# Causal maxima of four heads in four 32-row groups, three PSUM bank pairs, and the order of the steps as tables

## The chip, the core and the metric

The kernel runs on one core of a Trainium2 chip. The time is the device time of one execution in microseconds, the median of three runs. One execution was recorded by the hardware profiler; all rows below are from it. In its rows PE is TensorE's matmuls and PEld its weight loads, DVE is VectorE, ACT ScalarE, POOL GpSimd, and SP the queue that issues the DMAs.

## What is computed

Two transformer layers work on a tensor of 8 batches, 512 tokens and 128 channels. Every part normalises its input per token and adds its output to the residual.

1. A linear attention with 16 heads of 64 channels (`K` and `Q` are `elu + 1`, their sums over the tokens, a reciprocal, an output projection, a gelu).
2. A feed-forward part with three weights of 352 x 128, whose inputs and weights are quantised to FP4 in blocks of 16 and put back.
3. A causal softmax attention with 16 heads of 8 channels:

```python
a = jnp.einsum('bqhd,bkhd->bhqk', q, k) / Dh ** 0.5
a = jnp.where(jnp.tril(jnp.ones((1, 1, Lq, Lq), bool)), a, NEG_INF)
a = jax.nn.softmax(a, axis=-1)
o = jnp.einsum('bhqk,bkhd->bqhd', a, v)
```

4. A mixture of eight experts of low rank, of which two are chosen for each token.

The change is in part 3, and in how the instructions of all parts are ordered.

## The kernel before

**A plan.** The functions of `block_kernel` don't issue instructions. Through `nc` (an `Nc` over a `Plan`, lines 135 to 408) every call becomes a step with its engine, or `either`, which may be VectorE or GpSimd. `Plan.ordered` (line 249) then runs the steps in a model with a cost for each (`cost`, line 613), a rank for each stage (`TURNS`, line 706) and a pool of slots for each kind of tile. It picks for each engine the ready step of lowest rank, and so sets the order on every queue, the slot of every tile and the engine of every `either` step. `one_go` makes several calls one step, `together` lets a run of matmuls wait for all that they need. `kept_warm` (line 365) puts matmuls with zeros (`plan.warmer`, line 907) into gaps of TensorE that the model has. `Plan.issue` (line 397) emits the result. All of these instructions have line 407 in the profile, so the rows are told apart by tile.

**Stages.** For each batch: `normed_T`, `linear_attention` with `linear_out`, `fp4_feed_forward`, `causal_attention`, `routed`, `experts` (loop at line 1496). Stages of different batches are mixed. The elementwise products of `products` (`r`, `qf`), `quantised` (`qa`, `xf`, `hq`), `linear_out` (`y`) and `experts` (`act`, `um`) are `either` steps, 392 in all.

**PSUM.** Eight banks: two pairs (`pair`, 2 x 512 floats), one bank `mid` for the product with the values, three banks `ahead` for all else. `ahead` may also borrow halves of a pair.

**The causal attention.** Heads go in groups of four, 32 groups in all (`NG` = 4 a batch). A group's queries and keys lie in two tiles `qkT`, called `duo(n, i)` for `i` = 0, 1, in each of which head `h` = 0, 1 stands at partitions 64`h` to 64`h` + 31 (`stack`, line 1191). The 32 rows are high and low parts of 8 channels. `spread` (line 1195) loads them from HBM, where `projected` put them.

`group(n)` (line 1286) has two parts mixed in one loop over four blocks `t` of 128 tokens. For the next group, `largest` (line 1210) computes the maximum over the keys for each query: matmuls of 32 rows over the first 128(`t` + 1) keys, a matmul that adds the mask `mask_q` (a 128 x 128 bfloat16 tile of 0 and -1e30, multiplied by an identity) to the block on the diagonal, and a reduction on VectorE straight from PSUM. For t = 0 and 1 all four heads fit in one pair; for t = 2 and 3 two tiles take a pair each, one after the other (`shared`, line 1206). `to_queries` (line 1236) turns the maxima, in two parts, into two rows that are stored by DMA under the queries at partitions 64`h` + 32 and 33, so that the scores come out of the matmul with the maximum subtracted. For its own group, `scores` (line 1255) has matmuls over these 34 rows, an exponential on ScalarE (`pr`), and a select on GpSimd that clears what lies above the diagonal; then four matmuls with the values go side by side into four column groups of `mid`.

```python
for at, i in enumerate(some):
    for h in range(2):
        nc.tensor.matmul(heads[:, h, at, :], duo(n, i)[stack(h), 0, ts(t, P)],
                         duo(n, i)[stack(h), 1, 0:w], start=(at == 0), stop=False, ...)
for h in range(2):
    nc.tensor.matmul(heads[:, h, :, ts(t, P)], ident16,
                     mask_q.unsqueeze(1).to_broadcast([P, k, P]), start=False, stop=True, ...)
```

`first_maxima` (line 1342) fills the `qkT` tiles' key halves with ones and makes the maxima of group 0.

Of the kernel before, what the change touches and what calls it, by code (L numbers as in the profile page):

```python
# [9 lines left out]
F32 = mybir.dt.float32  # L10
F32R = mybir.dt.float32r
BF16 = mybir.dt.bfloat16
U32 = mybir.dt.uint32
AF = mybir.ActivationFunctionType
# [97 lines left out]
class Buf:  # L112


    def __init__(self, tag=None, place=None):
        self.tag, self.place = tag, place
        self.writer, self.readers = None, []
        self.first, self.users = None, {}


class Step:


    def __init__(self, number, engine, lane):
        self.number, self.engine, self.rank, self.lane = number, engine, 0.0, lane
        self.calls, self.needs, self.takes, self.uses = [], {}, [], {}
        self.cost, self.slow, self.port, self.size = 0.0, 0.0, False, 0
        self.work = 0.0
        self.start = self.end = None


TWO_PORTS = ("tensor_tensor", "scalar_tensor_tensor", "tensor_scalar", "tensor_copy")


class Plan:
# [3 lines left out]
    HOP = {"tensor": 0.1, "gpsimd": 0.1, "vector": 0.1, "scalar": 0.1, "sync": 0.2}  # L139

    def __init__(self, nc):
        self.nc, self.steps, self.open = nc, [], None
        self.lane, self.tags, self.psum, self.warmer = None, {}, (), None
        self.parts = {}
        self.engines = {n: Engine(self, n) for n in (*self.HOP, "either")}


    def tag(self, name, places, parts=None):

        self.tags[name] = list(places)  # L150
        self.parts[name] = parts or [((name, i),) for i in range(len(places))]
# [24 lines left out]

    def fixed(self, place):
        return View(Buf(place=place), place.shape)

# [4 lines left out]
    def together(self):  # L184
        return Together(self)

    def span(self, lane, low, high):
        return Span(self, lane, low, high)

    def add(self, engine, method, a, k):  # L190
        step = self.open
        if step is None:
            step = Step(len(self.steps), engine, self.lane)
            self.steps.append(step)
        elif step.engine is None:
            step.engine = engine
        assert step.engine == engine
        out = [k["out"]] if "out" in k else [a[0]]
        ins = [x for x in (*a[0 if "out" in k else 1 :], *k.values()) if isinstance(x, View)]
        if k.get("accum_out") is not None:  # L200
            out.append(k["accum_out"])
        step.calls.append((method, a, k))
        fast = "vector" if engine == "either" else engine
        if method is not None:
            step.cost += cost(fast, method, out[0], ins, a, k)
        if engine == "tensor" and method is not None:
            step.work += work(method, ins, a, k)
        if engine == "sync":
            step.size += 4 * out[0].shape[0] * _free(out[0])
        if engine == "either":  # L210
            step.slow += cost("gpsimd", method, out[0], ins, a, k)

        if engine == "gpsimd" and method != "memset":
            step.port = True
        elif engine in ("vector", "either") and method in TWO_PORTS:
            two = sum(v.shape[-1:] != (1,) or len(v.shape) > 2 for v in ins) > 1
            step.port |= (two or _free(out[0]) > 16) and not any(
                v.buf.tag in self.psum for v in (*ins, out[0]) if isinstance(v, View)
            )
        for v in ins:  # L220
            if all(v is not o for o in out) and isinstance(v, View):
                self.reads(step, v.buf)
        for v in out:
            if isinstance(v, View):
                self.writes(step, v.buf)

    def reads(self, step, buf):
        assert buf.writer is not None or buf.tag is None
        if buf.writer is not None and buf.writer is not step:
            step.needs[buf.writer] = True  # L230
        buf.readers.append(step)
        self.used(step, buf)

    def writes(self, step, buf):
        for s in (buf.writer, *buf.readers):
            if s is not None and s is not step:
                step.needs[s] = True
        buf.writer, buf.readers = step, []
        if buf.first is None and buf.tag is not None:
            buf.first = step  # L240
            step.takes.append(buf)
        self.used(step, buf)

    def used(self, step, buf):
        buf.users[step] = True
        step.uses[buf] = True


    def ordered(self):

        free = Free(self.parts)
        slots = {}
        left = {s: len(s.needs) for s in self.steps}
        then = {s: [] for s in self.steps}
        for s in self.steps:
            for n in s.needs:
                then[n].append(s)
        users = {}  # L260
        for s in self.steps:
            for b in s.uses:
                users[b] = len(b.users)
        ready_at = {s: 0.0 for s in self.steps}
        empties = set()
        for s in self.steps:
            for b in s.uses:
                if b.tag in self.psum and s.engine != "tensor" and (False or max(b.users, key=lambda u: u.number) is s):
                    empties.add(s)
        waiting = {e: [] for e in self.engines}  # L270
        for s in self.steps:
            if not left[s]:
                waiting[s.engine].append(s)
        turns = {}
        for s in sorted(self.steps, key=lambda s: (s.rank, s.number), reverse=True):
            for b in s.takes:
                turns.setdefault((s.lane, b.tag), []).append(b)
        busy = dict.fromkeys(self.engines, 0.0)
        port = 0.0
        moved = 0.0  # L280
        ends = []
        now, done, order, stuck = 0.0, 0, [], False
        clock = Clock()
        while done < len(self.steps):
            for e in self.HOP:
                while busy[e] <= now:
                    best, kept = None, set()
                    shared = waiting["either"] if e in ("vector", "gpsimd") else []
                    ready = [s for s in (*waiting[e], *shared) if ready_at[s] <= now]
                    ahead = HURRY if e == "tensor" and clock.idle(now) else 0.0  # L290
                    for s in sorted(
                        ready,
                        key=lambda s: (s.rank - (ahead if s.work > 0.6 * s.cost else 0.0) - (EMPTY if s in empties else 0.0), s.number),
                    ):
                        if s.port and port > now:
                            continue
                        asked = {}
                        for b in s.takes:
                            asked.setdefault(b.tag, []).append(b)
                        if not all(  # L300
                            all(b in turns[s.lane, t][-len(bs) :] for b in bs)
                            for t, bs in asked.items()
                        ):
                            continue
                        if all(
                            (t not in kept or stuck) and free.has(t, len(bs)) for t, bs in asked.items()
                        ):
                            best = s
                            break

                        kept.update(asked)
                    if best is None:
                        break
                    if any(
                        now < ready_at[s] <= now + PATIENCE and s.rank < min(best.rank - MARGIN, LIMIT)
                        for s in (*waiting[e], *shared)
                    ):
                        break
                    s, stuck = best, False
                    waiting[s.engine].remove(s)  # L320
                    if s.engine == "either":
                        s.engine = e
                        s.cost = s.slow if e == "gpsimd" else s.cost
                    for b in s.takes:
                        slots[b] = free.take(b.tag)
                        turns[s.lane, b.tag].remove(b)
# [1255 lines left out]
```

## Time and profile before

| | |
|---|---|
| time, median of 3 runs | 1126.88 us (1125.94 to 1127.14) |
| span of the profiled execution, first to last instruction | 1130.1 us, 3.2 us above the median |
| maxima: matmuls 32 rows | 512 instructions |
| maxima: mask matmuls | 384 instructions, 61.6 us busy |
| maxima: reductions `mx<-pair` on VectorE | 192, 198.5 us busy |
| fills with zeros | 88 instructions (44 fills), 40.4 us busy |
| `qf<-qf,r` and `qf<-qf,z`, 128x512, on GpSimd | 128, mean 1.27 us |
| `act<-act,tw`, 128x512, on GpSimd | 64, mean 1.27 us |
| `y<-y,y`, 128x512, on VectorE | 8, mean 0.73 us |
| `sc<-h`, reduction of 128x704, on VectorE | 14, mean 0.88 us |

How to read it: the page gives each engine's busy time, the chain of waits that ended last, and groups of instructions by tile, as `out<-in`. `x4` is a count. An fp32 matmul of 128 rows is two instructions. Matmuls overlap their neighbours, so a matmul's own duration is longer than the distance to the next one's start. The timeline merges like instructions that follow one another into one line with a count. A stretch's granted clock is the share of TensorE's full clock.

### The profile page before, as it was taken

How to read it: one execution, taken by the hardware profiler on the slowest of the kernel's cores; microseconds unless marked ns; L12 is line 12 of the kernel's file. 1: busy time of each engine (PE TensorE's matmuls, PEld its weight loads, DVE VectorE, ACT ScalarE, POOL GpSimd, SP SyncE). 2: the span in 40 equal slices, each digit the busy share in tenths (PEclk: the TensorE clock that was granted, in tenths of full speed). 3: DMA queues.
4: the chain of work that ended last, by engine and by line, in shares of the span. 5: the costliest groups of instructions: out<-in, count | busy, mean ns of one | idle time of the engine just before them, and what ended most of it. 6: DMA issues, size and time to landing. Idle time of an engine off the chain costs nothing.

```text
span 1130.1 us, 15043 instructions
## 1 busy us (share of the span) xinstructions
PE 1040.2 (92%) x5025; PEld 488.0 (43%) x5025; DVE 830.3 (73%) x1868; ACT 630.8 (56%) x1084; POOL 624.3 (55%) x669
## 2 busy tenths in 40 slices
PE   6667788998899999999998999999999999999998
PEld 2223333344344444444543444454454445445454
DVE  6868879897888967758788968788667765556543
ACT  5756787678786644644578555764443443344311
POOL 6647846676676466237635755467644533441534
PEclk9879989999999999999999999999999999999999
DMA  8000030001101020111012000210002102001000
GB/s 235 1 1 0 1 111 1 21 20 56 39 20 30 10 94 20 58 72 35 26 39 94 19 21 20 95 30 19 20 7 98 39 20 104 21 20 30 1 10 9
DMA packets 30572, 44.31 MB, mean 39 GB/s; under 512 B 4192, under 2 KB 18464, under 8 KB 30496
## 3 DMA queue, kind: packets, MB, share of 16 engines
q1 hardware_dynamic: 30496, 43.37, 11.9%
q8 instruction: 39, 0.64, 0.2%
q14 instruction: 37, 0.30, 0.1%
HBM read 23.95 MB, written 18.87 MB: 38 GB/s over the span
## 4 chain that ended last, share of the span: by engine, by line
PE 57%; DVE 15%; ACT 6%; issue 2%; POOL 1%; DMA 0%; POOLq 0%; DVEq 0%; ACTq 0%
PE ahead L407 31%; PE pair L407 19%; PE mid L407 7%; ACT pr L407 2%; DVE r L407 2%; DVE mx L407 2%; DVE h L407 1%; DVE sc L407 1%; ACT qf L407 1%; DVE s4 routing L407 1%; DVE qf L407 1%; DVE act L407 1%; ACT z L407 1%; DVE kf L407 1%; DVE oh L407 1%
## 5 line engine op out<-in xcount | busy, mean ns | idle before, releaser
L407 ACT ACTIVATE pr<-pair 128x1024 f32<-128x1024 f32 (+1 forms) x192 | 166.7, 879 | 149.2 <-PE pair L407 129.1
L407 DVE TENSOR_REDUCE mx<-pair 128x4 f32<-128x512 f32 (+2 forms) x192 | 198.5, 1041 | 68.4 <-PE pair L407 57.7
L407 POOL TENSOR_SCALAR_AFFINE_SELECT pr<-pr 128x256 f32<-128x256 f32 (+1 forms) x192 | 92.8, 485 | 176.4 <-ACT pr L407 175.6
L407 PE MATMUL pair<-qkT 32*128 32x128 f32 (+7 forms) x1024 | 172.3, 387 | 9.4 <-ACT pr L407 2.7
L407 PEld LDWEIGHTS pair<-qkT 32*128 32x128 f32 (+1 forms) x1024 | 84.4, 183 | 181.8 <-ACT pr L407 52.0
L407 POOL TENSOR_TENSOR act<-act,tw 128x512 f32<-128x512 f32 x64 | 81.3, 1272 | 88.8 <-DVE act L407 80.6
L407 PE MATMUL ahead<-um,b_sb 128*128 128x512 f32 x240 | 122.2, 607 | 0.0
L407 DVE RECIPROCAL r<-r 128x256 f32<-128x256 f32 x64 | 110.3, 1736 | 14.9 <-POOL r L407 14.8
L407 DVE SCALAR_TENSOR_TENSOR act<-act,ahead 128x512 f32<-128x512 f32 x120 | 81.9, 684 | 51.4 <-ACT act L407 38.0
L407 POOL TENSOR_TENSOR qa<-qa,qa 128x704 f32<-128x704 f32 (+4 forms) x60 | 81.2, 1354 | 35.1 <-DVE qa L407 26.2
L407 POOL TENSOR_TENSOR qf<-qf,r 128x512 f32<-128x512 f32 x64 | 80.5, 1278 | 34.5 <-DVE r L407 27.8
L407 PE MATMUL mid<-pr,va 128*10 128x512 f32 (+3 forms) x1024 | 93.3, 435 | 0.0
L407 POOL TENSOR_TENSOR qf<-qf,z 128x512 f32<-128x512 f32 x64 | 80.3, 1270 | 0.0
L407 ACT ACTIVATE act<-ahead 128x512 f32<-128x512 f32 x60 | 35.8, 597 | 72.0 <-PE ahead L407 71.9
L407 PE MATMUL ahead<-act,a_sb 128*128 128x512 f32 x128 | 65.2, 619 | 0.0
L407 POOL TENSOR_TENSOR r<-z,z 128x512 f32<-128x512 f32 x32 | 40.9, 1278 | 41.6 <-ACT z L407 39.3
L407 PE MATMUL ahead<-tT,w_sb 128*128 128x512 f32 x120 | 63.3, 609 | 0.0
L407 ACT ACTIVATE ahead<-ahead,bqkv_sb 128x512 f32<-128x512 f32 x96 | 63.0, 656 | 0.0
L407 PE MATMUL pair<-mask_q,ident 128*128 128x128 bf16 (+1 forms) x384 | 61.6, 242 | 0.0
L407 PE MATMUL ahead<-xnT,wk 128*128 128x512 f32 x100 | 56.7, 650 | 4.8 <-DVE kf L407 2.1
L407 PEld LDWEIGHTS ahead<-um,b_sb 128*128 128x128 f32 x240 | 40.7, 190 | 36.1 <-issue 29.6
L407 ACT ACTIVATE z<-qf,eps_sb,s 128x512 f32<-128x512 f32 x64 | 51.9, 811 | 6.8 <-DVE s L407 5.1
(227 smaller groups left out, 1986.4 us busy)
## 6 DMA issues: line engine op xcount, KB each, us to landing
stacks<-qk SPq DMA_DIRECT2D x32, 512.0 KB
qkT<-stacks SPq DMA_DIRECT2D x128, 128.0 KB
x<-in SPq DMA_DIRECT2D x8, 256.0 KB
qkT<-mr SPq DMA_DIRECT2D x128, 4.0 KB
out<-x SPq DMA_DIRECT2D x8, 256.0 KB
w_sb<-in SPq DMA_DIRECT2D x3, 256.0 KB
wq<-in SPq DMA_DIRECT2D x4, 128.0 KB
wk<-in SPq DMA_DIRECT2D x4, 128.0 KB
```

The costliest lines, as they stand in the source:

```text
L407: getattr(e, method)(*a, **k)
```

## The change

**Four row groups.** Head (`i`, `h`) now stands at partitions 64`h` + 32`i` of tile `duo(n, i)`, so the four heads of a group lie in four 32-row groups. `largest` takes two pairs at once, and each head has a bank of its own. It is called for t = 1, 2, 3; the call for t = 1 does t = 0 too, with 384 columns a head, of which the middle 128 are t = 0. The maxima of t = 1 come out in two parts, and `to_queries` joins them with a minimum (the maxima are negated).

```diff
-    def stack(h):
-        return slice(64 * h, 64 * h + 32)
+    def stack(i, h):
+        return slice(64 * h + 32 * i, 64 * h + 32 * i + 32)
...
+        t = max(t, 1)
+        some = (1, 0) if t == 1 else (t,)
+        w = sum((u + 1) * P for u in some)
+        pairs = [new("pair", [P, 2, 512]) for _ in range(2)]
+        four = [(i, h) for h in range(2) for i in range(2)]
+        with one_go():
+            for u in some:
+                for i, h in four:
+                    to, keys = pairs[i][:, h, 0:w], duo(n, i)[stack(i, h), 1, 0 : (u + 1) * P]
...
+                    nc.tensor.matmul(
+                        to, duo(n, i)[stack(i, h), 0, ts(u, P)], keys,
+                        start=(u == t), stop=False, skip_group_check=True,
+                    )
+            k = len(some)
+            for i, h in four:
+                nc.tensor.matmul(
+                    pairs[i][:, h, w - k * P : w].rearrange("p (k c) -> p k c", k=k),
+                    mask_q[stack(i, h)],
+                    mask_k[stack(i, h)].unsqueeze(1).to_broadcast([32, k, P]),
+                    start=False, stop=True, skip_group_check=True,
+                )
+        for i in range(2):
...
+            nc.vector.tensor_reduce(to, heads, AX.X, ALU.max, negate=True)
...
+        nc.vector.tensor_tensor(mx[:, :, 2], mx[:, :, 2], mx[:, :, 0], ALU.min)
```

The rows of the maxima go to the free half of each 64 partitions: 64`h` + 32 for `i` = 0 as before, 64`h` for `i` = 1. There the scores' matmul takes 64 rows, of which 30 hold zeros that `first_maxima` puts there once: the two odd tiles get eight fills in place of two.

```diff
-                        rows = slice(64 * h, 64 * h + 34)
+                        rows = slice(64 * h, 64 * h + (64 if i else 34))
```

**The mask as two factors.** `mask_q` and `mask_k` are bfloat16 tiles of 128 x 128 whose product over 32 rows gives the causal mask; each 32-row group holds the same rows. `causal_factors` makes them at the start, ahead of the other constants, with ten iotas on GpSimd and fifteen steps on VectorE on tiles of at most 150 columns, in one scratch tile (`pr`). It takes the place of a memset and a select on GpSimd.

**PSUM.** Three pairs, one bank `mid`, one bank `ahead`. `ahead` may use the six halves of the pairs.

```diff
-    places("pair", [P, 2, 512], 2, pool=sums)
+    places("pair", [P, 2, 512], 3, pool=sums)
...
-    places("ahead", [P, 512], 3, pool=sums)
+    places("ahead", [P, 512], 1, pool=sums)
```

**Tables.** The model, its costs, ranks and slots are gone. `ORDER` lists the 5108 steps in the order in which they are issued, two signs a step; `ENGINES` names an engine for each of the 392 `either` steps (126 `v`, 266 `g`); `PLACES` gives the slot of each tile; `ZEROS` names 15 fills by their place in the order (36 to 1394) and columns (192 to 512).

```diff
-        plan.issue()
+        plan.issue(ORDER, ENGINES, PLACES, ZEROS)
```

By stage the 126 are: 35 in the linear attention and its gelu, 48 in the FP4 part, 43 in the experts.

## The prediction

> **What bounds the kernel now.** I read the page's busy shares first, then the chain that ended last, then the busy time of each engine in three stretches, then TensorE's timeline inside an attention group.
>
> ```profile
> PE 1040.2 (92%) x5025; PEld 488.0 (43%) x5025; DVE 830.3 (73%) x1868; ACT 630.8 (56%) x1084; POOL 624.3 (55%) x669
> ...
> PE 57%; DVE 15%; ACT 6%; issue 2%; POOL 1%; DMA 0%; POOLq 0%; DVEq 0%; ACTq 0%
> ```
>
> The chain is mostly TensorE, and VectorE comes next. The stretches are cut at the first maxima matmul (172.0 us) and behind the last maxima (1036):
>
> ```profile
> 0.00:172.00 172.00, 126.68 (x313) 54.43 (x313) 129.35 (x348) 117.77 (x210) 106.34 (x130) 0.91 0.19 57
> 172.00:1036.00 864.00, 826.81 (x4385) 391.13 (x4385) 656.79 (x1430) 491.72 (x839) 479.71 (x505) 1.00 0.12 39
> 1036.00:1130.10 94.10, 86.76 (x331) 42.42 (x330) 44.18 (x92) 21.28 (x37) 38.21 (x35) 0.98 0.02 6
> ```
>
> The columns are stretch, length, then busy time of PE, PEld, DVE, ACT, POOL, then the granted clock. Ahead of the attention no engine is full (PE 127, DVE 129 of 172). In the middle TensorE is busy 827 of 864 us: 37 us are left, and another 18.3 us of its busy time are the fills with zeros. All maxima lie in this stretch, so this is where the change has to be priced. VectorE is busy 657 of 864 there (76%).
>
> **Maxima on TensorE.** One group of heads in TensorE's timeline, columns start and duration:
>
> ```profile
> 650.69 0.44 PE L407 MATMUL pair<-qkT 32*128 32x128 f32 x4
> 651.06 0.39 PE L407 MATMUL pair<-mask_q,ident 128*128 128x256 bf16 x2
> 651.29 1.08 PE L407 MATMUL ahead<-aout_sb,oT 128*128 128x128 f32 x8
> ...
> 654.46 0.50 PE L407 MATMUL pair<-qkT 32*128 32x256 f32 x4
> 654.90 0.39 PE L407 MATMUL pair<-mask_q,ident 128*128 128x256 bf16 x2
> ...
> 659.00 0.44 PE L407 MATMUL pair<-qkT 32*128 32x384 f32 x2
> 659.37 0.28 PE L407 MATMUL pair<-mask_q,ident 128*128 128x128 bf16 x2
> 659.49 0.66 PE L407 MATMUL ahead<-wT,hqT 128*128 128x128 f32 x4
> ...
> 662.67 0.50 PE L407 MATMUL pair<-qkT 32*128 32x512 f32 x2
> 663.11 0.28 PE L407 MATMUL pair<-mask_q,ident 128*128 128x128 bf16 x2
> ```
>
> Matmuls are pipelined, so a cost is the distance from one start to the next. Before: t=0 takes 651.06 - 650.69 = 0.37 for scores and 651.29 - 651.06 = 0.23 for the mask, 0.60. t=1 takes 0.44 + 0.23 = 0.67. t=2 takes 0.37 + 0.12 = 0.49, twice, 0.98. t=3 takes 0.44 + 0.12 = 0.56, twice, 1.12. Sum 3.37 us a group, 108 us for 32 groups. Two heads already run beside each other: two matmuls of 512 columns together take the 0.44.
>
> After: the four heads stand in four row groups and four banks. If four run beside each other as two do now, t=3 is 0.44 and t=2 is 0.37; the joined t=1 and t=0 take half of 0.44 and half of 0.37, 0.41. The masks are now four 32-row matmuls of 256, 128 and 128 columns that run together; I give them what two mask matmuls of that width take now, 0.23 + 0.12 + 0.12 = 0.47, though they may take half, 0.23. Sum 0.44 + 0.37 + 0.41 + 0.47 = 1.69 us, a saving of 1.68 x 32 = **54 us**.
>
> Four row groups at once are not in this trace, so both ends: if only two go at a time, scores stay at 0.37 + 0.44 + 0.74 + 0.88 = 2.43, and masks two by two cost 0.47: saving 0.47 x 32 = 15 us. With masks at half, 62 us. A loss on TensorE is excluded by the rows: two row groups do overlap, and no column is added. I take 54, because the nearest rows overlap fully: two row groups here, and four column groups in the product with the values.
>
> The page "TensorE: Matmul & The Clock Gate" of the Trainium skill, "Measured speedup vs the span model", speaks against full overlap: four row tiles at 512 columns gave 3.07 times, not four. By it a four-way step costs 4/3.07 = 1.30 of the trace's overlapped one, an estimate: scores 1.22 become 1.59, and 12 us of the gain are lost.
>
> The scores' matmuls for the odd tile contract 64 rows where they contracted 34; the columns are the same and the row of 34 costs what the row of 32 costs (0.44 at 384 columns): nothing, cover not needed.
>
> **Fills.** Before has 44 (88 instructions, 40.4 us busy, 17.2 / 18.3 / 5.0 in the three stretches); the table has 15, all within the first 1394 of 5108 steps. They stand in gaps, so leaving them out gives nothing by itself and at most 18 in the middle. What they cover is the granted clock (1.00 in the middle); a stretch at 0.86, as at 50 to 100 us, would cost about 14% of itself. TensorE is so full there that I put nothing.
>
> **Elementwise steps.** All 392 steps that may go to either engine run on GpSimd now. The table sends 126 to VectorE: 24 before the first maxima, 91 in the middle, 11 behind. VectorE has no such row with two SBUF tensors but y<-y,y (0.73 us at 512 columns; 0.68 mostly); for 704 columns I take the reduction sc<-h, 0.88. Middle: 71 x 0.73 + 20 x 0.88 = 70 us more on VectorE; GpSimd loses 71 x 1.27 + 20 x 1.5 = 120. The new minimum over two parts is 32 x 0.17 = 5 us (row s4 routing, 128x4); it sits ahead of the maxima's copy and their DMA, a group ahead of use. The number of reductions and their elements per group are equal (5120). So VectorE in the middle goes from 657 to 732. The fullest 50 us that it shows (350 to 400) are 45.85, 92%; at 92% it needs 732 / 0.92 = 796 us. TensorE needs 864 - 54 = 810. TensorE still ends last, by little. Bounds: nothing, if VectorE keeps up, to the second rival's price.
>
> **Start.** The mask's factors are made by 10 iotas and 15 small VectorE steps that alternate through one scratch tile; the old mask took two GpSimd steps. By rows of 0.29 (affine select, 128 columns) and about 0.2 (small VectorE steps), 10 x 0.29 + 15 x 0.2 = 6 us one after another; the six further fills of qkT cost some 2 us (0.36 each for the wide ones). All of it stands ahead of the first statistics at 5.16 on VectorE's queue, and GpSimd's pow is behind the iotas; the weights' loads on SP run meanwhile. Between 0, if it hides behind the first load, and 8; I take 5, as everything waits for the first normalised tile.
>
> **Banks.** The three pairs are a further slot for the maxima and scores; one own bank, and borrowed halves, are left for everything else. Total banks are equal. Now TensorE's loads waited 33.9 us in 52 cases for a reduction and 53.1 us in 91 for an exponential, but TensorE itself stood only 2.0 and 2.7 us for them. Both ends: a quarter of the 55 us of gaps and fills in the middle gained, or the third rival's loss. I take 10 us gained, from the freer pairs and from moved steps that end 0.6 us sooner.
>
> The table's order keeps the stretches' content: the same linear parts of three batches ahead of the first maxima; behind the last maxima all 54 TensorE steps of the last experts and 47 of 54 of the ones before, where the trace now has all of both. So 172 and 94 stay.
>
> **Sum.** 1130.1 - 54 + 5 - 10 = 1071 on the profiled span. That span is 1.003 of the median 1126.9, so 1068.
>
> **Rivals.**
>
> *Better than that.* TensorE gets the 62 us, the start hides, and the gaps and fills of the middle shrink by 30 of 55: 1130 - 62 - 30 = 1038, 1035 on the median's scale. For it: no engine is full in the first 172 us and the steps are freer. Against: VectorE at 657 + 75 = 732 would have to be busy 94% of the 778 us left.
>
> *VectorE becomes the bound.* The copy and subtraction of the maxima show what VectorE suffers beside GpSimd:
>
> ```profile
> L407 DVE CAST m<-mx x32: 174/175/987, 185.6 to 1036.3; 128x16 fp32r<-128x16 f32 x32
> L407 DVE TENSOR_TENSOR m<-mx,m x32: 105/175/1245, 188.2 to 1036.5; 128x16 fp32r<-128x16 f32 x32
> ```
>
> The same 175 ns step takes up to 1.25 us; its mean of 281 ns is 0.11 over the median. GpSimd, with 480 - 120 = 360 us left in some 810, would be busy 44% of the time, and a step that met one of its 1.27 us steps half way waits 0.64: 0.44 x 0.64 = 0.28. At 0.3 us for each of the 91 moved steps VectorE would need (732 + 27) / 0.92 = 825 us: 172 + 5 + 825 + 94 = 1096, 1093. The page "SBUF — State Buffer", "SBUF: two separate sides", says that a VectorE step with two SBUF inputs and a GpSimd step exclude each other for a whole instruction; by it each such wait may last GpSimd's 1.27 us, which fits the maximum of 1.25. If two row groups at a time is all there is, the answer is 1130 - 15 + 5 = 1120, 1117.
>
> *Slower.* Each of the 96 maxima blocks takes two pairs, four of the seven shared banks, and frees the second only when two reductions (0.95 to 1.22 us each) are through. If TensorE then waits for one reduction a block, that is 96 x 1.04 = 100 us: 1130 - 54 + 5 + 100 = 1181, 1178. It decides from a wait of 0.5 us a block on. Against it: the 2.0 us of such waits now, with two pairs only. That the fixed order itself stands badly to the chip would look the same, as waits of TensorE.
>
> **Chances.** Forecast 0.45, better 0.22, VectorE 0.18, two at a time 0.05, slower 0.08, no change 0.02. A measurement of this kernel can tell about 0.2%. Faster 0.90, same 0.02, slower 0.08. The range that leaves out no more than two in ten goes from the better case to beyond the VectorE case: 1031 to 1101.
>
> **What would show it.** Right: the four 32-row matmuls start within some 20 ns, a t=3 block costs 0.5 to 0.6 us in place of 1.12, TensorE's busy time falls to about 955, VectorE's rises to about 925, and GpSimd's falls to about 465. Wrong: four heads that start two by two; TensorE waiting for mx; VectorE above 93% in the middle with TensorE idle behind it; a clock below 0.97 behind 300 us, where no fills are left; a first statistics step after 15 us.

## The result, and the profile after

The changed kernel takes 1267.39 us (median of four runs, 1263.94 to 1273.39) where the one before took 1127.01 beside it: ratio 1.123, 95 % interval 1.118 to 1.127. It is 12 % slower; the forecast was 1068. The profiled execution took 1267.84 us, with a span of 1266.1.

The page of the changed kernel: busy shares, the granted clock in 40 slices, and the chain that ended last.

```profile
PE 1029.0 (81%) x4967; PEld 482.4 (38%) x4967; DVE 913.6 (72%) x2047; ACT 636.3 (50%) x1084; POOL 485.8 (38%) x551
...
PEclk9898979989989999889979998999998889996999
...
PE 20%; DVE 10%; ACT 4%; issue 1%; POOL 1%; DVEq 0%; ACTq 0%; POOLq 0%
```

VectorE (913.6; "about 925") and GpSimd (485.8; "about 465") came out close to the forecast. TensorE did not: 1029.0 us busy in place of 955, at a granted clock that stands below 0.9 in 13 of the 40 slices (3 before), and only 81 % of the span. No engine is full. The chain's known shares add up to 36 %; before, to 81 %.

The three stretches of the changed kernel, cut at its first maxima matmul (194.60) and behind its last maxima (1169); columns as in the prediction.

```profile
0.00:194.60 194.60, 128.99 (x305) 55.82 (x305) 148.39 (x402) 119.28 (x214) 92.04 (x116) 0.89 0.16 49
194.60:1169.00 974.40, 817.31 (x4338) 386.33 (x4341) 717.25 (x1547) 495.85 (x836) 368.26 (x412) 0.92 0.11 35
1169.00:1266.10 97.10, 82.65 (x329) 40.28 (x321) 47.99 (x101) 21.17 (x36) 25.48 (x24) 0.96 0.02 6
```

The loss is in the first two stretches: 194.6 us for 172.0, and 974 for 864. In the middle TensorE stands 157 us (it stood 37), and the clock is 0.92 where it was 1.00. The idle time of TensorE in the waits of the changed kernel (us in total, times, longest):

```profile
PE pair L214 <- DVE act L214: 32.7, 31, 3.2
PE pair L214 <- DVE qf L214: 22.4, 14, 3.5
PE pair L214 <- DVE pair L214: 18.0, 10, 4.4
PE pair L214 <- ACT pr L214: 15.0, 33, 3.1
PE pair L214 <- ACT pair L214: 15.0, 8, 4.1
PE pair L214 <- DVE mx L214: 12.7, 26, 2.2
```

The largest are not the maxima (`mx`, 12.7 us). They are matmuls into a `pair` that wait for a VectorE step that has just *read* a `pair`: the experts' product into `act`, the linear attention's sum into `qf`.

TensorE's time from one start to the next, summed by kind over the records, with its idle time apart (us; "one tile" is the experiment that decided the case, below):

| | before | after | after, one tile |
|---|---|---|---|
| maxima, masks | 77.1, 39.0 | 35.7, 24.2 | 35.3, 23.7 |
| fills | 37.8 | 16.6 | 15.7 |
| all other matmuls | 886 | 951 | 886 |
| idle | 82.3 | 227.7 | 100.3 |
| of it, waits for a reader of the pair's other half | 7 | 121 | 2 |
| busy at half clock, by the clock's records | 33 | 176 | 64 |

So maxima and masks gave up 56 us, as forecast (54). Idle time took 145, and the other matmuls grew by 65, which fits the clock: 176 us of TensorE's busy time ran at half clock (33 before), and (176 - 33) / 2 = 72 us. The row of the other half is worked out as follows: each instruction of the trace was matched with its call in the order table, so that for each matmul it is known when its operands were written, when its own half was last read, and when the other half was. What is counted is time in which TensorE was free, operands and own half were ready, and the start came only when a reader of the *other half* had ended. By the same count such time went from 26 to 60 us on ScalarE and from 22 to 54 on VectorE: readers wait for the other half's writer as well.

One of these, TensorE in the changed kernel:

```profile
835.11 0.59 PE L214 MATMUL pair<-tT,w_sb 128*128 128x512 f32 x1
835.54 1.02 PE L214 MATMUL pair<-um,b_sb 128*128 128x512 f32 x2
839.73 1.39 PE L214 MATMUL pair<-xnT,wv 128*128 128x512 f32 x2 [3.17 <-DVE qf L214]
```

and VectorE at that time:

```profile
835.71 3.35 DVE L214 RECIPROCAL r<-r 128x256 f32<-128x256 f32 x2
838.98 0.10 DVE L214 SCALAR_TENSOR_TENSOR s4 attention<-mv attention,s4 attention 128x4 f32<-128x4 f32 x1
839.00 0.68 DVE L214 SCALAR_TENSOR_TENSOR qf<-pair,qf 128x512 f32<-128x512 f32 x1
```

The projection of the values needs `xnT` and `wv`, ready long since. It goes to half 0 of pair 0, which nobody uses. Half 1 of the same pair waits for VectorE, which is in two reciprocals. TensorE is free from 836.56; the matmul starts at 839.73, 50 ns after `qf` has been read out of half 1. The reading is that the program orders a write to a tile behind the readers of that tile, and that a pair is one tile; "One tile for all of PSUM", below, tests it. The case costs 3.17 us on TensorE, and behind it, from 840.46 on, the clock's records show half clock for 3.4 us.

### The profile page after: what moved, and what is told of

It reads as the page before. It is cut to its first block, busy times and chain, and to the rows that moved or that the text cites. A ratio compares the mean times of both kernels' runs of the same rounds, so it can differ in the third digit from the quotient of the medians.

```text
span 1266.1 us, 14915 instructions
## 1 busy us (share of the span) xinstructions
PE 1029.0 (81%) x4967; PEld 482.4 (38%) x4967; DVE 913.6 (72%) x2047; ACT 636.3 (50%) x1084; POOL 485.8 (38%) x551
## 5 line engine op out<-in xcount | busy, mean ns | idle before, releaser
L214 DVE TENSOR_REDUCE mx<-pair 128x6 f32<-128x768 f32 (+2 forms) x192 | 193.1, 1037 | 44.7 <-PE pair L214 43.1
L214 PE MATMUL pair<-qkT 32*128 32x128 f32 (+11 forms) x1024 | 143.7, 410 | 34.7 <-ACT pr L214 12.9
L214 PEld LDWEIGHTS pair<-qkT 32*128 32x128 f32 (+2 forms) x1024 | 72.2, 197 | 179.7 <-ACT pr L214 56.8
L214 PE MATMUL pair<-um,b_sb 128*128 128x512 f32 x192 | 102.2, 630 | 22.0 <-DVE act L214 15.4
L214 DVE SCALAR_TENSOR_TENSOR act<-act,pair 128x512 f32<-128x512 f32 x96 | 65.0, 683 | 71.5 <-ACT act L214 39.1
L214 PE MATMUL pair<-xnT,wv 128*128 128x512 f32 x106 | 59.8, 650 | 22.5 <-DVE qf L214 11.0
L214 PE MATMUL pair<-xnT,wk 128*128 128x512 f32 x100 | 61.4, 707 | 18.4 <-ACT pair L214 6.3
L214 PE MATMUL pair<-xnT,wq 128*128 128x512 f32 x100 | 57.7, 662 | 16.6 <-DVE pair L214 4.4
L214 PE MATMUL pair<-qf,wk_o 128*128 128x512 f32 x96 | 55.7, 699 | 17.4 <-ACT pair L214 5.5
L214 ACT ACTIVATE pair<-pair,bqkv_sb 128x512 f32<-128x512 f32 x100 | 65.6, 658 | 6.6 <-PE pair L214 5.8
```

The costliest lines, as they stand in the source:

```text
L214: getattr(e, method)(*a, **k)
```

## The experiments

First theories: **tables** (the fixed order stands badly to the chip), **banks** (fewer own banks, blocks that take two pairs), **engines** (the moved elementwise steps) and **clock** (the missing fills). The theory that won, **shared tile**, came out of the first four runs and the trace.

### The change without its tables

The changed maxima, mask factors and banks in the kernel before, whose own planner makes the order and chooses the fills (its costs of the 32-row matmuls are adjusted); all `either` steps run on GpSimd. Then the same with the banks of before.

```diff
-    places("pair", [P, 2, 512], 2, pool=sums)
-    places("ahead", [P, 512], 3, pool=sums)
+    places("pair", [P, 2, 512], 3, pool=sums)
+    places("ahead", [P, 512], 1, pool=sums)
```

> The changed maxima, mask factors and three bank pairs, but ordered by the model of the kernel before (which also picks fills, slots and engines) in place of the tables. Theory 'tables' (the fixed order doesn't fit the chip, so TensorE waits and its clock falls): TensorE waits below 120 us, clock above 0.97, time 1070 to 1110. Theory 'banks' (two pairs at a time and one own bank make TensorE wait in any order): 1180 or more. Theory 'clock' (too few fills): as 'tables', since the model puts fills.

Measured: 1226.29 us, ratio 1.085 (1.082 to 1.088).

> As x1, but with the banks of the kernel before, two pairs and three own ones: a maxima block then takes both pairs. 'tables': 1080 to 1130, a little slower than x1, since scores have to wait while a block holds both pairs. 'banks': if the single own bank was the fault, faster than x1 by 30 us or more; if the two pairs at a time were, slower than x1 by 30 or more.

Measured: 1209.62 us, ratio 1.069 (1.068 to 1.071). With another order the kernel is still 158 and 142 us above the forecast: the tables by themselves are not the cause. With two pairs TensorE's loads wait more for the reductions (73.4 us in 101 cases against 35.9 in 51), yet the kernel is faster than with three. That spoke against the third rival as the main cause. Waits of TensorE for the other half, counted as above: 46 us with three pairs, 11 with two.

### All either steps on GpSimd

```diff
-ENGINES = (
-    "ggvgvvggvgggggvvgggggvvvvggvgggggggvggvgggvgvvvvgvvggggggggggggggvggggggggggvggggggggggg"
...
-)
+ENGINES = "g" * 392
```

> The changed kernel with all 392 steps of free engine on GpSimd, the tables of order, slots and fills untouched. If the 126 steps on VectorE are what TensorE waits for ('engines'): 1180 or less. 'tables': the order was made for the other split, so no gain, 1260 to 1310.

Measured, in one run: 1269.11 us where the table's split took 1267.39. The engines are not it.

### More fills

The changed kernel with 142 fills in place of 15, in gaps that its trace shows.

> The changed kernel with 142 fills in place of 15, put where TensorE stood for over 0.45 us in its trace. 'clock': granted clock 0.97 or more, and the 199 us at half clock (176 us of them with TensorE busy, so 88 us lost) mostly go: 1185 to 1205. 'tables' alone, with waits that don't depend on the clock: clock up, but time above 1230.

Measured, in one run: 1229.33 us, clock 0.972 in place of 0.922. The higher clock, less the time of the fills that hold it up, is worth 38 us, short of what theory 'clock' expected; idle time and fills together are still 275 us (244 without these fills).

### One tile for all of PSUM

If all of PSUM is taken as one tile, the compiled program was expected to order a matmul behind the readers of its own banks only. So the same tables, engines, places, banks and instructions can be run with one thing changed:

```diff
-    places("pair", [P, 2, 512], 3, pool=sums)
-    places("mid", [P, 512], 1, pool=sums)
-    places("ahead", [P, 512], 1, pool=sums)
+    banks = sums.tile([P, 8, 512], F32, name="banks", tag="banks")
+    plan.tag("pair", [banks[:, 2 * i : 2 * i + 2, :] for i in range(3)])
+    plan.tag("mid", [banks[:, 6, :]])
+    plan.tag("ahead", [banks[:, i, :] for i in range(7, 8)])
```

> The changed kernel with the same tables of order, engines and places; only the PSUM is taken as one tile of eight banks, and pairs, mid and the single bank are views of it. In such a tile the compiled program orders a matmul behind the readers of its own bank only; in a tile of two banks it orders it behind the readers of both. Theory 'shared tile' (steps that borrow half a pair wait for the reader of the other half; by the trace of the changed kernel 117 of 225 us of TensorE's waits over 0.1 us end that way, against 7 of 80 before): 1267 falls by 90 to 150, to 1117 to 1177, the clock rises above 0.95. Theory 'order' (the tables stand badly to the chip, and behind a false wait a true one is due soon): less than 30 us, 1237 to 1267. Theory 'two pairs at once' (maxima blocks wait for two reductions): no change beyond 1%.

Measured: **1075.40 us**, ratio 0.951 (0.948 to 0.953): 192 us less than the changed kernel, and 5 % faster than before. Its page:

```profile
PE 961.4 (90%) x4967; PEld 466.5 (44%) x4967; DVE 909.5 (85%) x2047; ACT 631.1 (59%) x1084; POOL 486.5 (45%) x551
...
DVE 44%; PE 40%; ACT 8%; issue 4%; POOL 2%; SPq 0%; DMA 0%; DVEq 0%; ACTq 0%; POOLq 0%
```

The same instructions take 68 us less of TensorE's busy time (half clock 64 us in place of 176), and the chain can be followed to the end. The waits that led the list of the changed kernel have shrunk from 32.7, 22.4 and 18.0 us, while the one for the maxima has not (12.7):

```profile
PE banks L214 <- DVE act L214: 3.1, 6, 0.7
PE banks L214 <- DVE qf L214: 3.9, 6, 1.5
PE banks L214 <- DVE banks L214: 5.6, 5, 2.5
PE banks L214 <- DVE mx L214: 16.4, 30, 2.6
```

The same projection, on TensorE with one tile:

```profile
705.16 1.02 PE L214 MATMUL banks<-um,b_sb 128*128 128x512 f32 x2
706.02 1.88 PE L214 MATMUL banks<-xnT,wv 128*128 128x512 f32 x4
```

and VectorE beside it:

```profile
704.38 1.69 DVE L214 RECIPROCAL r<-r 128x256 f32<-128x256 f32 x1
705.99 0.09 DVE L214 SCALAR_TENSOR_TENSOR s4 attention<-mv attention,s4 attention 128x4 f32<-128x4 f32 x1
706.01 0.67 DVE L214 SCALAR_TENSOR_TENSOR qf<-banks,qf 128x512 f32<-128x512 f32 x1
```

The matmul starts at 706.02, straight behind the one before it, while VectorE has only begun to read `qf`'s half (706.01 to 706.68). The same call of the order table waited 3.17 us in the changed kernel. So the ordering by whole tiles is shown, for a tile of two banks, by the one thing that was changed.

The same allocation for the kernel before, and for the two kernels under its planner:

> The kernel before with the same allocation of PSUM as one tile and nothing else. Theory 'shared tile': the trace of before shows 7 us of such waits, so 0 to 10 us faster, 1117 to 1127. The other theories: no change, 1127.

Measured: 1111.24 us, ratio 0.982 (0.980 to 0.984). Before lost some 20 us to it as well, more than the 7 us of direct waits on TensorE: its idle time fell by 10 us (82 to 72), and the time busy at half clock from 33 to 18, worth 7.

> The changed maxima and mask factors with three pairs and one single bank under the planner of before, PSUM as one tile. It took 1226 us with a tile for each pair; its trace showed 46 us of waits for the reader of the other half. Theory 'shared tile': 1160 to 1185, as the planner's own order was made for halves that are free of each other. Theory 'order': 1200 to 1226.

Measured: 1132.31 us, ratio 1.001 (0.999 to 1.002), 94 us less than with a tile for each pair, more than expected. It is still 21 us slower than the kernel before with one tile: maxima and masks take 57 us less, but the planner puts in 117 fills in place of 44 (49 us more), and TensorE's idle time is 28 us longer.

> The same with two pairs and three single banks, PSUM as one tile. It took 1210 us with a tile for each pair; its trace showed 11 us of waits for the reader of the other half. Theory 'shared tile': 5 to 15 us faster, 1195 to 1205: what is left here is the block that takes both pairs at once. If it falls below 1180, the loss with two pairs was the tile too.

Measured: 1185.32 us, ratio 1.048 (1.045 to 1.051), 24 us less, again more than expected. What is lost grows with the borrowing: 192 and 94 us with six borrowed halves and one own bank, 24 and 20 with four and three. Among kernels with one tile the tables beat the planner by 57 us at equal computation and banks (1075 against 1132), so the theory of the bad tables falls. And with two pairs the kernel takes 53 us more than with three. That would fit the prediction's slower rival, as TensorE's weight loads wait more for a reduction, in the kernel with two pairs

```profile
PEld banks L409 <- DVE mx L409: 72.6, 100, 3.2
```

and in the one with three

```profile
PEld banks L409 <- DVE mx L409: 41.3, 57, 2.2
```

It isn't shown, though. TensorE itself is idle for the same time in both (99 and 100 us). What differs is that the planner puts in 153 fills in place of 117 (121 us in place of 85), and that 64 us in place of 36 ran at half clock.

### With one tile: fills, engines, and what TensorE's time is worth

23 fills added to the kernel with one tile, in gaps just ahead of and inside its stretches at half clock (8960 columns).

```diff
+    501: 512,
+    513: 512,
...
+    4751: 320,
```

> The changed kernel with PSUM as one tile (ratio to before 0.951), with 23 more fills (8960 columns, some 15 us of TensorE) in gaps that its trace shows just ahead of and inside its 14 stretches at half clock; TensorE was busy 64 us in these, so the half clock cost 32 us. Theory 'clock' (fills of that kind are worth leaving in): half of the 32 us comes back, ratio 0.93 to 0.94, clock above 0.98. Theory 'fills at nothing' (as the prediction put it, what is gained in clock is lost to fills and to other engines): 0.946 to 0.956.

Measured: **1063.76 us**, ratio 0.941 (0.939 to 0.944): the fastest kernel of this study. The granted clock of the kernel with one tile, in 40 slices,

```profile
PEclk9998999999999999899999999999999999997999
```

and with the fills:

```profile
PEclk9998999999999999999999999999999999999999
```

Busy time at half clock falls from 64 to 14 us, and fills take 19 us more; the time falls by some 10 us.

> The same kernel with one tile, with all 392 steps that may go to either engine on GpSimd, as before the change. Here nothing false holds the engines, so the price of the moved steps is to be seen. Prediction's term 'elementwise steps at nothing': within 5 us of the one with the table's split, ratio 0.947 to 0.956. Theory 'the moved steps shorten chains' (each moved step ends 0.6 us sooner, 126 of them): 10 to 30 us slower, 0.96 to 0.98. Theory 'VectorE is the bound' (its 910 us of 1071): faster, below 0.945.

Measured: 1074.05 us, ratio 0.949 (0.947 to 0.951), with the edit shown under "All either steps on GpSimd". VectorE is 61 us less busy, GpSimd 141 more, and nothing moves.

The outer tile's maxima matmuls and the masks issued twice:

```diff
-                for i, h in four:
+                for i, h in four * (2 if u == t else 1):
...
-            for i, h in four:
+            for j, (i, h) in enumerate(four * 2):
```

> The same kernel with one tile, with the four matmuls of the outer tile of each maxima block and its four mask matmuls issued twice (the second pass writes the same maxima and adds the mask's large negative numbers once more, so the masked scores are twice as low). By their sums in the trace this adds some 50 us to TensorE's work: 1.1 us of scores and 0.74 of masks a group, 32 groups, less the overlap. Theory 'TensorE is the bound, so the maxima saved what they are worth': 40 to 55 us slower, ratio 0.985 to 1.0. Theory 'TensorE waits for VectorE and ScalarE around the blocks': below 25 us, under 0.973.

Measured: 1084.70 us, ratio 0.958 (0.956 to 0.960). The added passes took not 50 but 25 us of TensorE (maxima 35.3 to 54.3, masks 23.7 to 30.0), and 8 us of the time ((0.9580 - 0.9506) x 1132; 4 to 12 with both intervals).

Two row groups at a time, as before the change:

```diff
-        four = [(i, h) for h in range(2) for i in range(2)]
+        four = [(i, h) for i in range(2) for h in range(2)]
+        half = [slice(64 * h, 64 * h + 64) for h in range(2)]
...
-                        to, duo(n, i)[stack(i, h), 0, ts(u, P)], keys,
+                        to, duo(n, i)[half[h], 0, ts(u, P)], keys,
...
-                    mask_q[stack(i, h)],
+                    mask_q[half[h]],
```

> The changed kernel with PSUM as one tile (ratio to before 0.951), but each maxima matmul and each mask matmul contracts 64 rows in place of 32, so that only two heads run beside each other, as before the change; columns, banks, order and reductions stay (the second head's rows are added in, so the maxima are not those of the heads; two fills of 512 columns are added at the start). TensorE's own work should rise from 35 to some 70 us for the maxima and from 24 to some 40 for the masks, 50 us in all. Prediction's term 'maxima on TensorE, all of it on the path': 45 to 55 us slower, ratio 0.99 to 1.0. Theory 'half of it hides behind VectorE and ScalarE' (the doubled passes added 25 us to TensorE and 9 to 14 to the time): 18 to 32 us slower, 0.967 to 0.979. Below 0.96: the maxima's saving is worth next to nothing, and the order tables made the kernel with one tile fast.

Measured: 1079.30 us, ratio 0.953 (0.950 to 0.957), not to be told from the kernel with four row groups (0.951). TensorE's work rose by only 17 us: maxima and scores together 113.5 to 130.0, masks the same (23.6). "50 us in all" was wrong, so the run doesn't price the whole saving: it shows that 17 us more of TensorE's work cost next to nothing here. That the tables made the kernel with one tile fast, not the row groups by themselves, is the reading that fits, with 1132 us under the planner and 1075 with the tables; which part of the tables does it is not shown.

## Why the prediction was wrong, step by step

**"Banks. ... I take 10 us gained, from the freer pairs and from moved steps that end 0.6 us sooner": the step that failed.** It counted banks ("total banks are equal") and not tiles. Before, everything but the attention had three banks of its own and borrowed halves now and then; after, it has one and six halves, so most of the work shares a tile with a neighbour that it has nothing to do with. In place of 10 us gained, 192 us were lost, shown by the one allocation that takes the loss away (1267 to 1075). The profile before held the hint in little: 7 us of TensorE's waits were of this kind. Both ends of the term ("a quarter of the 55 us of gaps ... or the third rival's loss") left it out.

**"Fills ... TensorE is so full there that I put nothing": failed with it.** The reason was sound only while TensorE is full. With 157 us of holes in the middle the clock there was 0.92, and 142 fills won back 38 us. Even with one tile, where TensorE is 90 % busy, 23 fills won 10. The sign "a clock below 0.97 behind 300 us" came out: 0.93 in the changed kernel.

**"Maxima on TensorE ... a saving of 54 us": the size held, in part by luck; its worth did not.** One block of t = 3 and one of t = 2, TensorE in the changed kernel:

```profile
715.84 0.50 PE L214 MATMUL pair<-qkT 32*128 32x512 f32 x4
716.18 0.23 PE L214 MATMUL pair<-mask_k,mask_q 32*128 32x128 bf16 x4
...
730.71 0.45 PE L214 MATMUL pair<-qkT 32*128 32x384 f32 x4 [0.27 <-DVE mx L214]
730.99 0.24 PE L214 MATMUL pair<-mask_k,mask_q 32*128 32x128 bf16 x4
```

The four start within 10 ns of each other (0, 4, 7 and 10 in the records), and the masks follow 0.34 us later at 512 columns; before, two heads took 0.43. A t = 3 block takes 0.57 us in the median, 0.51 with one tile. The total of 56 us is right beside 54, but not its parts: by the prediction's rows the maxima go from 78 us to 39 and the masks from 30 to 15, and measured were 77 to 36 and 39 to 24. Nor is most of it owed to four heads abreast: with two row groups at a time TensorE's work in the kernel with one tile rose by only 17 us, so that some 40 of the 56 us would be saved even so, where the prediction had 15 for that case. What saves the rest (blocks joined, masks of 32 rows in place of 128) no run separates. "TensorE: Matmul & The Clock Gate", "Measured speedup vs the span model", in the Trainium skill gives 3.07 times for four row tiles at 512 columns, and by the estimate from it the maxima would have taken 1.59 x 32 = 51 us. They took 36, so that loss is not seen here. But the sum took the whole saving as time. With the order held, 25 us more of TensorE's work cost 8 us and 17 us more cost 3 (within the intervals nothing): TensorE waits for others around the blocks anyhow (the idle time fell from 100 us to 94 and 97). What the maxima bring is then probably not 54 us but a part, which no run here isolates.

**"Elementwise steps ... nothing": right**, under both allocations (1269 against 1267; 0.949 against 0.951). The second rival, VectorE as the bound, did not come, though the chain with one tile gives VectorE 44 %. Its single waits did last as long as feared: the longest copy `m<-mx` took 1.29 us, median 0.17.

**"Start ... I take 5": near.** The first statistics step starts at 11.4 us, 5.2 before, so 6.2 later. What that costs the whole is not shown: with one tile the first stretch is 17 us shorter than before, not longer.

**"So 172 and 94 stay": wrong.** The kernel with one tile, cut in the same way:

```profile
0.00:155.30 155.30, 117.08 (x305) 52.05 (x305) 146.47 (x400) 116.98 (x211) 91.97 (x115) 0.96 0.20 62
155.30:989.00 833.70, 766.74 (x4338) 375.17 (x4341) 714.22 (x1548) 493.19 (x838) 369.13 (x413) 0.97 0.12 41
989.00:1071.10 82.10, 77.58 (x329) 39.26 (x321) 48.77 (x101) 20.95 (x36) 25.44 (x24) 1.00 0.03 7
```

Its span, 1071.1, is the forecast's 1071 to the microsecond, but not by the forecast's way: forecast were 177 (172 and the start's 5), 800 (864 less 64) and 94, and they came out 155, 834 and 82. The middle is 34 us too long, the ends 34 too short, and the sum agrees because the errors cancel: that is luck, and the run doesn't confirm the terms.

**The better rival** has a slip: "the 778 us left" should be 864 - 62 - 30 = 772, and VectorE's share 95 %, which speaks against it a little more.

**The slower rival** had the side right, at 0.08, but not the mechanism. Waits of TensorE for `mx` are 12.7 us in 26 cases in the changed kernel, not 100 us in 96, and 16.4 in 30 with one tile, where the kernel is fast. Its other clause, "that the fixed order itself stands badly to the chip", is refuted as put: with one tile for PSUM the same order is the fastest one here.

What stays open: how much of the 57 us between the tables and the planner comes from which choice in the tables, and how the kernel before would stand with tables of its own.

## What to carry to other kernels

When small results borrow pieces of a larger buffer, ask what the program tracks: bytes, banks or the tile. If it is the tile, every lodger waits for its neighbour's readers, and no count of free banks shows it; in the trace it looks like a matmul, with its operands long ready, that starts 50 ns after a step that read something else. Before pricing fewer instructions as fewer microseconds, issue them twice and see how much of the added work shows in the time: here 8 of 25 us.

## What the runs showed of the hardware that was not expected

A second pass over the same operands is much cheaper than the first: maxima take 35.3 / 32 = 1.10 us a group, 0.97 of it for the outer tiles, and these issued again added 19.0 / 32 = 0.59. Two 64-row groups in place of four 32-row groups raised the maxima by 17 us of 35, not by 35, and left the masks at 23.6. In the kernel before, the same two-by-two maxima took 77 us, in smaller blocks of one pair with 128-row masks in between.

The granted clock falls to half in stretches of 3.4 us and their multiples. Within the spans these are 8 stretches (41 us) before, 35 (198 us) after, 13 (68 us) with one tile, 5 (14 us) with 23 more fills. In the changed kernel the holes in TensorE's work cost half as much again in clock as they cost themselves: 72 us more of lost clock beside 145 more of idle time, though the engine was still 81 % busy.
